# Cross-attention of a perceiver block: Newton steps on VectorE for the inverse roots, earlier loads of the second group's x, and a first group in two halves

## The chip, the cores and the metric

The kernel runs on one core of one Trainium2 chip. The metric is device time in microseconds (us) of one execution; the number compared is the median over several executions. The engines are named as the profile names them: PE (TensorE matmuls), PEld (TensorE weight loads), DVE (VectorE), ACT (ScalarE), POOL (GpSimd), SP (the queue that issues most DMAs).

## The reference

The block computes three residual steps on `x` of 128 batches x 32 rows x 512 columns, float32. The change lies in the first one alone: a layer norm of `x`, then cross-attention of each batch's 32 rows over 257 rows of context plus the 32 rows themselves.

```python
def _layernorm(x, axis=-1, eps=1e-05):
    m = jnp.mean(x, axis=axis, keepdims=True)
    v = jnp.var(x, axis=axis, keepdims=True)
    return (x - m) / jnp.sqrt(v + eps)

def _L0_xattn_ref(x, mask, k_cache, v_cache, wq, wk, wv, wo):
    q = jnp.einsum('bsd,ed->bse', x, wq)
    k_new = jnp.einsum('bsd,ed->bse', x, wk)
    v_new = jnp.einsum('bsd,ed->bse', x, wv)
    k = jnp.concatenate([k_cache, k_new], axis=1)
    v = jnp.concatenate([v_cache, v_new], axis=1)
    scale = 1.0 / math.sqrt(q.shape[-1])
    scores = jnp.einsum('bqd,bkd->bqk', q, k) * scale
    attn = jax.nn.softmax(scores, axis=-1)
    out = jnp.einsum('bqk,bkd->bqd', attn, v)
    return jnp.einsum('bqd,ed->bqe', out, wo)

x = x + _L0_xattn_ref(_layernorm(x), mask, ctx_2048, ctx_2048, wq, wk, wv, wo)
x = x + _L0_attn_ref(_layernorm(x), ...)   # delta-rule attention and an MLP
x = x + _L0_ffn_ref(_layernorm(x), ...)    # Hadamard FFN with quantised weights
```

## The kernel before

`perceiver_block` runs four stages one after the other: `cross_attention`, `delta_products`, `delta_out_mlp` and the Hadamard FFN. Only `cross_attention` is touched. It takes about the first 665 us of the span.

**Tiles and groups.** The 4096 rows of `x` are cut into 32 tiles of 128 rows (4 batches each), and the tiles into 8 groups of 4 (`SG = 512` rows). A tile's load is `load_x` (line 244, 256 KB). For each group `s` the normed rows are turned into `hT` (columns on partitions, 512 rows along the free axis), and `hT` is multiplied by `wq` and `wk` in 512-wide matmuls (line 437) into `qT` and `kT`. These are four output chunks `ec` of four partial products `dc` for each weight; every float32 matmul shows as two MATMUL records.

**One tile of attention.** For tile `n` the loop issues, in program order: `new_rows` (the tile's own values, L314, and the DMAs that put them beside the last context row in `vx`), `turned` (transposes of the softmax weights of tile `n-1`, L358), `project` of tile `n-2` (L395), `values` of tile `n-1` (L371 and L378, then the scaling `ao`, L383), `weights` of tile `n` (scores L336, maximum `nms` L341 and L342, exponential L346), and `flipped` (transposes of `ao`, L97). Context comes in two transfers of 2 MB a tile, `kall` for the keys (`load_keys`, L290) and `cx` for the values (`load_values`, L296), in two buffers each. A tile's `kall` is requested two tiles ahead, and a tile's `cx` one tile ahead, each as soon as the older buffer has been read.

**The norm of the next group.** `prepared(s + 1, ...)` is a generator that is advanced twice in each tile. Its steps for group `s+1` are: load of x tiles 0 to 2; an empty step; load of x tile 3 and mean and variance (L81, L82) of tiles 0 to 2; mean and variance of tile 3 and the inverse roots; the normed rows `xn` (L250) of the four tiles and their transposes (`across`: L97 on PE, then a copy into `hT` on ACT, L254). The inverse root is `deviation` (L258: a Sqrt activation on ACT over four columns) and a `reciprocal` on DVE (L276).

**The first group** has nothing to hide behind. It runs tile by tile, with the order on DVE written out by hand through `InOrder` (each instruction gets an edge to the one before it): statistics of tile `i`, Sqrt on ACT, then reciprocal, `xn` and transposes of tile `i-1`. Only then do the first matmuls with `wq` start.

**Order of the rest.** Outside `InOrder` the framework's scheduler sets each engine's order when the program is built: among the instructions that its own timing calls ready, the one that comes first in the program goes first. Beside the attention, `quantised_weights` reads the FFN's weights (`raw`, L192, 256 KB each), takes their absolute sums (L197) and rounds them (L212 to L214) on DVE; it is advanced four times a tile. DMAs of SP start in the order of its queue.

**The order of the initial loads** on SP is: x tiles of group 0, `wq`, `wk`, `wv`, `kall` and `cx` of tile 0, `wo`, `kall` and `cx` of tile 1.

Of the kernel before, what the change touches and what calls it, by code (L numbers as in the profile page):

```python
# [9 lines left out]

FP = mybir.dt.float32
BF = mybir.dt.bfloat16
AF = mybir.ActivationFunctionType
ALU = mybir.AluOpType
# [4 lines left out]
P = 128  # L19
D = 512  # L20
DC = D // P
NB = 128
T = 32
NT = NB * T
# [5 lines left out]
SG = 512  # L30
# [5 lines left out]
LN_EPS = 1e-5  # L36
RMS_EPS = 1e-6
Q_EPS = 1e-5
MAGIC = 12582912.0


def bc(ap, n):
# [15 lines left out]
class Ctx:  # L58


    def __init__(self, ctx, tc):
        self.tc, self.nc = tc, tc.nc
        nc = self.nc
        const = ctx.enter_context(tc.tile_pool(name="const", bufs=1))
        self.ident = const.tile([P, P], FP, name="ident")
        make_identity(nc, self.ident)
        self.identb = const.tile([P, P], BF, name="identb")
        nc.vector.tensor_copy(self.identb, self.ident)
        self.ones = const.tile([P, P], FP, name="ones")
        nc.vector.memset(self.ones, 1.0)  # L70
        self.ln_eps = const.tile([P, 1], FP, name="ln_eps")
        nc.vector.memset(self.ln_eps, LN_EPS)
        self.rms_eps = const.tile([P, 1], FP, name="rms_eps")
        nc.vector.memset(self.rms_eps, RMS_EPS)
        self.eps2 = const.tile([P, 1], FP, name="eps2")
        nc.vector.memset(self.eps2, LN_EPS * RMS_EPS)

    def mean_var(self, dve, pool, x, mv):

        st = pool.tile([P, 6], FP, name="bn_st")  # L80
        dve.bn_stats(st, x)  # L81
# [99 lines left out]
def quantised_weights(g: Ctx, pool, st, ps, out, weights):  # L181
# [3 lines left out]
    for (src, dst), sc in zip(weights, out):  # L185
# [23 lines left out]
        for i, piece in enumerate(pieces):  # L209
            t = load(piece)  # L210
            q = pool.tile([P, D], BF, name="qw")
            nc.vector.tensor_scalar(t, t, inv, 1.0, ALU.mult, ALU.min)  # L212
            nc.vector.tensor_scalar(t, t, -1.0, MAGIC, ALU.max, ALU.add)
            nc.vector.tensor_scalar(q, t, MAGIC, None, ALU.subtract)  # L214
            nc.gpsimd.dma_start(dst[:, i * D : (i + 1) * D], q)
# [3 lines left out]
def cross_attention(g: Ctx, x, ctx_kv, ctxT, wqT, wkT, wvT, woT, x1, stats, scales, ffn_weights):  # L219
# [5 lines left out]
    tc, nc = g.tc, g.nc  # L225
# [5 lines left out]
    with stack:  # L231
# [9 lines left out]
        def load_x(s, i):  # L241
            t = xp.tile([P, D], FP, name="xt")
            r = s * SG + i * P
            nc.sync.dma_start(t, x[r : r + P, :])
            return t

        def normed(dve, xt, mv, rstd):

            xn = wk.tile([P, D], FP, name="xn")
            dve.tensor_scalar(xn, xt, mv, rstd, ALU.subtract, ALU.mult)  # L250
            return xn

        def across(hT, i, xn):
            nc.scalar.copy(hT[:, :, i * P : (i + 1) * P], g.transposed(ps, xn, g.ident))  # L254

        def deviation(mv, n):
            rstd = st.tile([P, n], FP, name="rstd")
            nc.scalar.activation(rstd, mv[:, :, 1], AF.Sqrt, bias=g.ln_eps)  # L258
            return rstd

        def prepared(s, xt, hT):

            n = SG // P
            xt.extend(load_x(s, i) for i in range(n - 1))
            yield
            mv = st.tile([P, n, 2], FP, name="mv")
            yield
            xt.append(load_x(s, n - 1))  # L270
            for i in range(n - 1):
                g.mean_var(nc.vector, st, xt[i], mv[:, i, :])
            yield
            g.mean_var(nc.vector, st, xt[n - 1], mv[:, n - 1, :])
            rstd = deviation(mv, n)
            nc.vector.reciprocal(rstd, rstd)  # L276
            yield
            xn = []
            for i in range(n + 2):
                if 2 <= i:  # L280
                    across(hT, i - 2, xn[i - 2])
                if i < n:
                    xn.append(normed(nc.vector, xt[i], mv[:, i, 0:1], rstd[:, i : i + 1]))
                if i % 2:
                    yield

        def load_keys(gi):

            kall = cp.tile([P, DC, 4, NK], FP, name="kall")
            nc.sync.dma_start(kall[:, :, :, 0:LC], ctxT[gi])  # L290
            return kall

        def load_values(gi):
            b0 = gi * 4
            cx = cp.tile([P, 4, 2, D], FP, name="cx")
            nc.sync.dma_start(  # L296
                cx.rearrange("p b r d -> p b (r d)"),
                ctx_kv[b0 : b0 + 4, 0 : LC - 1, :].rearrange("b (p r) d -> p b (r d)", r=2),
            )
            return cx  # L300
# [102 lines left out]
        xt = [load_x(0, i) for i in range(SG // P)]  # L403
        kalls, cxs, quantised = {}, {}, None
        soft, out = None, None
        w = {}
        for n, src, wp in (("q", wqT, wp1), ("k", wkT, wp1), ("v", wvT, wp2), ("o", woT, wp3)):
            w[n] = wp.tile([P, DC, D], FP, name=f"w{n}")
            load_rows(nc, w[n], src)
            if n == "v":  # L410
                kalls[0] = load_keys(0)
                cxs[0] = load_values(0)
        kalls[1] = load_keys(1)
        cxs[1] = load_values(1)

        hT = sp.tile([P, DC, SG], FP, name="hT")
        dve = InOrder(tc, nc.vector)
        got = []
        for i in range(SG // P + 1):
            if i < SG // P:  # L420
                mv = st.tile([P, 1, 2], FP, name="mv0")
                g.mean_var(dve, st, xt[i], mv[:, 0, :])
                got.append((mv[:, 0, 0:1], deviation(mv, 1)))
            if i:
                mv, rstd = got[i - 1]
                dve.reciprocal(rstd, rstd)
                across(hT, i - 1, normed(dve, xt[i - 1], mv, rstd))
        for s in range(NT // SG):
            if s == NT // SG - 1:
                g.factors(*(t[:, 0:EARLY] for t in stats))  # L430
            qT = sp.tile([P, DC, SG], FP, name="qT", bufs=1)
            kT = sp.tile([P, DC, SG], FP, name="kT", bufs=1)
            for wn, dst in ((w["q"], qT), (w["k"], kT)):
                for ec in range(DC):
                    pp = ps.tile([P, SG], FP, name="ps")
                    for dc in range(DC):
                        nc.tensor.matmul(
                            pp, wn[:, dc, ec * P : (ec + 1) * P], hT[:, dc, :],
                            start=dc == 0, stop=dc == DC - 1,
                        )  # L440
                    (nc.vector.tensor_copy if ec % 2 else nc.scalar.copy)(dst[:, ec, :], pp)

            if quantised is None:
                quantised = quantised_weights(g, qp, st, ps, scales, ffn_weights)
            xt_next, hT_next, ahead = [], None, iter(())
            if s + 1 < NT // SG:
                hT_next = sp.tile([P, DC, SG], FP, name="hT")
                ahead = prepared(s + 1, xt_next, hT_next)
            for i in range(SG // P):
                n = s * (SG // P) + i  # L450
                kall = kalls.pop(n)
                vx = new_rows(n, kall, hT, kT, i)
                if soft is not None:
                    m, xm, vm, pr, rs = soft
                    prT = turned(pr)
                if out is not None:
                    project(*out)
                    out = None
                if soft is not None:
                    ao = values(cxs.pop(m), vm, prT, rs)  # L460
                    if n + 1 < NT // P:
                        cxs[n + 1] = load_values(n + 1)
                for _ in range(2):
                    next(quantised, None)
                next(ahead, None)
                got = weights(kall, qT, i)
                if n + 2 < NT // P:
                    kalls[n + 2] = load_keys(n + 2)
                if soft is not None:
                    out = m, xm, flipped(ao)  # L470
                for _ in range(2):
                    next(quantised, None)
                soft = n, xt[i], vx, *got
                next(ahead, None)
            xt, hT = xt_next, hT_next
# [2 lines left out]
        project(m, xm, flipped(values(cxs.pop(m), vm, turned(pr), rs)))  # L478


NG = NT // SG
GT = SG // P
GB = SG // T
H4 = 4
NC8 = H // H4
# [717 lines left out]
class HadamardFfn:  # L1203
# [5 lines left out]
    NG = IF // D  # L1209
# [66 lines left out]
    def open(self, ctx):  # L1276
# [22 lines left out]
    def first(self, ps):  # L1299
# [3 lines left out]
        for i in range(2):  # L1303
# [15 lines left out]
    def run(self):  # L1319
# [330 lines left out]
```

## Time and profile before

| what | us |
|---|---|
| three timed executions | 2870.92, 2873.64, 2877.52 |
| median | 2873.64 |
| the profiled execution, first to last instruction (its span) | 2872.8 |
| PE busy in the span | 2793.6 (97%) |
| DVE, ACT, POOL busy | 2016.4, 1037.3, 728.4 |
| mean granted TensorE clock | 0.992 of full speed |

The page gives no time for the profiled execution beside its span. The span lies 0.8 us under the median and inside the range of the three timed executions. "Granted clock" is the share of TensorE's full clock that the throttle let through. A row of a timeline has a start, a duration, the engine, the line in the kernel, the operation, output and inputs, a count, and in brackets the idle time of that engine before it with what ended the idle time.

### The profile page before, as it was taken

To read this page: it belongs to the slowest core of one execution; us is meant where nothing else is said; L and a number is where in the kernel's file an instruction comes from. 1 tells how busy PE (TensorE), PEld (TensorE's weight loads), DVE (VectorE), ACT (ScalarE), POOL (GpSimd) and SP (SyncE) were. 2 spreads that over 40 slices of the span, in tenths; PEclk is the share of its full clock that TensorE was granted. 3 is DMA by queue.
4 is the path that set the end of the run, shared out by engine and by line. 5 is a ranking of instruction groups with operands and counts; after the bars stand their busy time and mean duration, and the time that the engine had idled before them with its cause. 6 is when DMAs were issued, how large, how long until landed. Compare 5 with 4: busy or idle time off the path is not lost.

```text
span 2872.8 us, 45044 instructions
## 1 busy us (share of the span) xinstructions
PE 2793.6 (97%) x16863; PEld 1675.9 (58%) x16926; DVE 2016.4 (70%) x3371; ACT 1037.3 (36%) x1791; POOL 728.4 (25%) x1098
## 2 busy tenths in 40 slices
PE   8999999999999999899999999999999989999998
PEld 4444444444444444667676767677777656666665
DVE  2453544426599999778787777878622289999998
ACT  1111111215666666312222221111211146667665
POOL 2232323322687786221211121101100000000000
PEclk9999999999999999999999999999999999999999
DMA  9798998874555666641424231322221124443443
GB/s 325 260 328 303 347 334 287 298 250 120 160 145 143 185 181 186 188 130 58 133 62 129 67 124 54 120 85 65 95 88 34 35 76 88 88 87 83 85 82 76
DMA packets 347178, 429.80 MB, mean 150 GB/s; under 512 B 151888, under 2 KB 252624, under 8 KB 344528
## 3 DMA queue, kind: packets, MB, share of 16 engines
q1 hardware_dynamic: 305952, 324.36, 37.1%
q0 software_dynamic: 41008, 102.55, 11.7%
q8 instruction: 135, 2.21, 0.3%
q14 instruction: 83, 0.68, 0.1%
HBM read 288.88 MB, written 94.37 MB: 133 GB/s over the span
## 4 chain that ended last, share of the span: by engine, by line
PE 59%; DVE 13%; issue 2%; DMA 1%; SPq 0%; ACT 0%; POOL 0%; DVEq 0%; POOLq 0%; ACTq 0%
PE ps L151 19%; PE pm L1083 10%; PE pm L1086 9%; PE pm L1094 9%; PE pp L151 5%; PE ps L1057 4%; DVE acc L151 3%; PE ps L1026 2%; DVE W L151 2%; DVE pr L535 1%; DVE W L541 1%; DVE pr L151 1%; PE pg L151 1%; DMA xs<-x 1%; DVE m L151 1%
## 5 line engine op out<-in xcount | busy, mean ns | idle before, releaser
L1083 PE MATMUL pm<-hT,wg 128*128 128x256 f32 x1408 | 342.5, 385 | 0.2 <-ACT hT L1072 0.2
L1086 PE MATMUL pm<-hT,wu 128*128 128x256 f32 x1408 | 336.3, 382 | 1.3 <-DVE wu L1144 1.3
L1094 PE MATMUL pm<-wd,mT 128*128 128x512 f32 x704 | 307.4, 592 | 0.0
L1086 PEld LDWEIGHTS pm<-hT,wu 128*128 128x128 f32 x1408 | 269.3, 191 | 39.1 <-DVE wu L1144 1.6
L1083 PEld LDWEIGHTS pm<-hT,wg 128*128 128x128 f32 x1408 | 262.5, 191 | 50.3 <-issue 10.0
L535 DVE TENSOR_TENSOR pr<-L,W 128x960 f32<-128x960 f32 (+30 forms) x201 | 238.4, 1186 | 7.6 <-DMA L<-ld 3.8
L541 DVE TENSOR_TENSOR W<-W,pr 128x1024 f32<-128x1024 f32 (+30 forms) x202 | 241.3, 1195 | 2.3
L1094 PEld LDWEIGHTS pm<-wd,mT 128*128 128x128 f32 x704 | 132.4, 190 | 160.2 <-issue 160.0
L151 PE MATMUL ps<-wq,qT 128*128 128x512 bf16 x930 | 217.2, 381 | 4.6 <-ACT t L151 3.0
L1088 ACT ACTIVATE sg<-pm 128x256 f32<-128x256 f32 x176 | 67.3, 383 | 336.9 <-PE pm L1083 327.0
L1089 DVE TENSOR_TENSOR mT<-pm,sg 128x256 f32<-128x256 f32 x176 | 74.0, 421 | 143.0 <-PE pm L1086 141.2
L1420 POOL DMA_DIRECT2D xo<-x x31 | 26.3, 849 | 525.2 <-ACT xo L151 490.8
L323 POOL DMA_DIRECT2D vx<-vn x256 | 126.3, 500 | 118.7 <-DVE vn L319 92.5
L151 PEld LDWEIGHTS <-qT 128*128 128x128 bf16 x960 | 94.4, 98 | 105.0 <-issue 6.1
L151 DVE TENSOR_TENSOR mb<-m 128x1024 f32<-128x1024 f32 x128 | 153.3, 1219 | 0.1
L151 DVE TENSOR_TENSOR m<-mb 128x1024 f32<-128x1024 f32 x128 | 150.8, 1220 | 1.2
L151 ACT ACTIVATE t<-ps,magic,qs 128x512 f32<-128x512 f32 x158 | 115.6, 780 | 42.7 <-DVE qs L151 38.9
L151 PEld LDWEIGHTS ps<-hd,mT 128*128 128x128 f32 x1024 | 120.8, 194 | 6.9 <-ACT mT L151 2.8
L151 PE MATMUL ps<-hd,mT 128*128 128x128 f32 x1024 | 121.3, 277 | 2.3 <-ACT mT L151 2.3
L151 PE MATMUL pp<-hT,wv 128*128 128x512 f32 x256 | 120.3, 614 | 0.0
L579 POOL TENSOR_TENSOR kk<-kk,cm 128x256 f32<-128x256 f32 x128 | 118.4, 925 | 2.7
L151 PE MATMUL pp<-hT,wk 128*128 128x512 f32 x256 | 116.2, 596 | 1.9 <-ACT hT L151 1.9
(236 smaller groups left out, 4877.8 us busy)
## 6 DMA issues: line engine op xcount, KB each, us to landing
kall<-in_ctxT_dram SPq DMA_DIRECT2D x32, 2056.0 KB
cx<-in_ctx_dram SPq DMA_DIRECT2D x32, 2048.0 KB
x<-xo POOLq DMA_DIRECT2D x64, 256.0 KB, 3.6
ld<-kk POOLq DMA_DIRECT2D x128, 128.0 KB, 2.9
pd<-kk POOLq DMA_DIRECT2D x128, 128.0 KB, 2.7
L<-ld SPq DMA_DIRECT2D x32, 512.0 KB
pe<-pd SPq DMA_DIRECT2D x256, 64.0 KB
kqm<-kq SPq DMA_DIRECT2D x448, 32.0 KB
```

The lines of the kernel that those rows point to most:

```text
L151: got = method(*args, **kw)
L323: nc.gpsimd.dma_start(vx[r : r + T, j, :], vn[j * T : (j + 1) * T, halves[h]])
L535: self.dve.tensor_mul(pr[:, 0:n], bc(L[:, s, :, s + 1 : T].rearrange("p h t -> p t h"), HD), w[:, s].unsqueeze(1).to_broadcast([P, n, H4, ...
L541: self.dve.tensor_sub(w[:, s + 1 :], w[:, s + 1 :], pr[:, 0:n])
L579: nc.gpsimd.tensor_mul(q, q, cm.unsqueeze(1).to_broadcast([P, 2 * H4, T]))
L1026: last["pe"] = nc.tensor.matmul(po[a * 32 : (a + 1) * 32, c, :].rearrange("p (j t) -> p j t", t=T), m[:, 4 * c + a, e, :], q[:, :, 2 * a + ...
L1057: nc.tensor.matmul(pw, oT[:, i, dc, :], wo[:, dc, :], start=dc == 0, stop=dc == DC - 1)
L1083: nc.tensor.matmul(pg, wg[:, dc, fs], hT[:, dc, :], start=dc == 0, stop=dc == DC - 1)
L1086: nc.tensor.matmul(pu, wu[:, dc, fs], hT[:, dc, :], start=dc == 0, stop=dc == DC - 1)
L1088: nc.scalar.activation(sg, pg, AF.Silu)
L1089: mark[:] = [nc.vector.tensor_mul(mT[:, fc, :], pu, sg).ins]
L1094: nc.tensor.matmul(pd, mT[:, fc, i * P : (i + 1) * P], wd[:, fc, :], start=fc == 0, stop=fc == FC - 1,)
```

## The change

Three things change in `cross_attention`.

1. `deviation` and the reciprocal after it are replaced, for groups 1 to 7, by `inverse_root`: a seed from integer arithmetic on the bits of variance plus epsilon, and three Newton steps, all on DVE (13 instructions on 128x4). Group 0 keeps Sqrt and reciprocal.
2. The four x tiles of group 1 are loaded at the start, between `wo` and the `kall` and `cx` of tile 1. `prepared` loads only what is not there yet; for groups 2 to 7 it loads as before.
3. Group 0 is worked in two halves of two tiles: statistics, roots, normed rows and transposes of tiles 0 and 1, then their part of `qT` in matmuls of 256 columns, then the same for tiles 2 and 3. The order on PE, ACT and DVE is now written out through `InOrder` (the copies of `qT` out of PSUM are not part of it). `kT` of group 0, and both of the later groups, stay 512 wide.

```diff
-        def across(hT, i, xn):
-            nc.scalar.copy(hT[:, :, i * P : (i + 1) * P], g.transposed(ps, xn, g.ident))
-
-        def deviation(mv, n):
-            rstd = st.tile([P, n], FP, name="rstd")
-            nc.scalar.activation(rstd, mv[:, :, 1], AF.Sqrt, bias=g.ln_eps)
-            return rstd
+        def across(hT, i, xn, pe=None, act=nc.scalar):
+            act.copy(hT[:, :, i * P : (i + 1) * P], g.transposed(ps, xn, g.ident, pe=pe))
+
+        def projected(pe, dst, wn, hT, ts):
+            for ec in range(DC):
+                pp = ps.tile([P, ts.stop - ts.start], FP, name="ps")
+                for dc in range(DC):
+                    pe.matmul(
+                        pp, wn[:, dc, ec * P : (ec + 1) * P], hT[:, dc, ts],
+                        start=dc == 0, stop=dc == DC - 1,
+                    )
+                (nc.vector.tensor_copy if ec % 2 else nc.scalar.copy)(dst[:, ec, ts], pp)
+
+        def inverse_root(mv, n):
+            h = st.tile([P, n], FP, name="h")
+            y, t = (st.tile([P, n], FP, name=k) for k in ("rstd", "rt"))
+            nc.vector.tensor_scalar(h, mv[:, :, 1], LN_EPS, None, ALU.add)
+            nc.vector.tensor_single_scalar(t.bitcast(INT), h.bitcast(INT), 1, ALU.logical_shift_right)
+            nc.vector.tensor_scalar(y.bitcast(INT), t.bitcast(INT), -1, SEED, ALU.mult, ALU.add)
+            nc.vector.tensor_scalar(h, h, -0.5, None, ALU.mult)
+            for _ in range(3):
+                nc.vector.tensor_mul(t, y, h)
+                nc.vector.tensor_mul(t, t, y)
+                nc.vector.scalar_tensor_tensor(y, t, 1.5, y, ALU.add, ALU.mult)
+            return y

         def prepared(s, xt, hT):
             n = SG // P
-            xt.extend(load_x(s, i) for i in range(n - 1))
+            xt.extend(load_x(s, i) for i in range(len(xt), n - 1))
             yield
             mv = st.tile([P, n, 2], FP, name="mv")
             yield
-            xt.append(load_x(s, n - 1))
+            xt.extend(load_x(s, i) for i in range(len(xt), n))
...
             g.mean_var(nc.vector, st, xt[n - 1], mv[:, n - 1, :])
-            rstd = deviation(mv, n)
-            nc.vector.reciprocal(rstd, rstd)
+            rstd = inverse_root(mv, n)
...
                 cxs[0] = load_values(0)
+        second = [load_x(1, i) for i in range(SG // P)]
         kalls[1] = load_keys(1)
         cxs[1] = load_values(1)
...
-        dve = InOrder(tc, nc.vector)
-        got = []
-        for i in range(SG // P + 1):
-            if i < SG // P:
-                mv = st.tile([P, 1, 2], FP, name="mv0")
-                g.mean_var(dve, st, xt[i], mv[:, 0, :])
-                got.append((mv[:, 0, 0:1], deviation(mv, 1)))
-            if i:
-                mv, rstd = got[i - 1]
-                dve.reciprocal(rstd, rstd)
-                across(hT, i - 1, normed(dve, xt[i - 1], mv, rstd))
+        pe, act, dve = (InOrder(tc, e) for e in (nc.tensor, nc.scalar, nc.vector))
+        qT = sp.tile([P, DC, SG], FP, name="qT", bufs=1)
+        for half in range(2):
+            tiles = range(half * GT // 2, (half + 1) * GT // 2)
+            mvs = [st.tile([P, 2], FP, name="mv0") for _ in tiles]
+            roots = [st.tile([P, 1], FP, name="root") for _ in tiles]
+            for i, mv, root in zip(tiles, mvs, roots):
+                g.mean_var(dve, st, xt[i], mv)
+                act.activation(root, mv[:, 1:2], AF.Sqrt, bias=g.ln_eps)
+            for i, mv, root in zip(tiles, mvs, roots):
+                dve.reciprocal(root, root)
+                across(hT, i, normed(dve, xt[i], mv[:, 0:1], root), pe, act)
+            projected(pe, qT, w["q"], hT, slice(half * SG // 2, (half + 1) * SG // 2))
...
             kT = sp.tile([P, DC, SG], FP, name="kT", bufs=1)
+            if s:
+                qT = sp.tile([P, DC, SG], FP, name="qT", bufs=1)
+                projected(nc.tensor, qT, w["q"], hT, slice(0, SG))
+            projected(nc.tensor, kT, w["k"], hT, slice(0, SG))
...
-            xt_next, hT_next, ahead = [], None, iter(())
+            xt_next, hT_next, ahead = [] if s else second, None, iter(())
```

More of the change, by code (lines that the diff above doesn't have):

```diff
@@ L11 @@
 FP = mybir.dt.float32
+INT = mybir.dt.int32
 BF = mybir.dt.bfloat16
@@ L39 @@
 MAGIC = 12582912.0
+SEED = 0x5F3759DF
+NG = NT // SG
+GT = SG // P
 def bc(ap, n):
@@ L430, in cross_attention @@
                 g.factors(*(t[:, 0:EARLY] for t in stats))
-            qT = sp.tile([P, DC, SG], FP, name="qT", bufs=1)
             kT = sp.tile([P, DC, SG], FP, name="kT", bufs=1)
[L433 to L441, printed above, removed]
+            if s:
+                qT = sp.tile([P, DC, SG], FP, name="qT", bufs=1)
+                projected(nc.tensor, qT, w["q"], hT, slice(0, SG))
+            projected(nc.tensor, kT, w["k"], hT, slice(0, SG))
             if quantised is None:
                 quantised = quantised_weights(g, qp, st, ps, scales, ffn_weights)
-            xt_next, hT_next, ahead = [], None, iter(())
+            xt_next, hT_next, ahead = [] if s else second, None, iter(())
             if s + 1 < NT // SG:
@@ L478, in cross_attention @@
         project(m, xm, flipped(values(cxs.pop(m), vm, turned(pr), rs)))
-NG = NT // SG
-GT = SG // P
 GB = SG // T
```

## The prediction

> **What bounds the kernel now.** I read the page's busy table first, then the windows of 20 us over the first 760 us, then PE's own waits in the cross-attention, and last the timeline around the longest of them.
>
> The windows show who sets the pace of this stage. Columns: length, busy us and count of PE, PEld, DVE, ACT, POOL, then granted clock, DMA share, GB/s.
>
> ```profile
> 0.00:20.00 20.00, 12.66 (x31) 6.74 (x32) 5.90 (x23) 5.18 (x10) 0.70 (x6) 1.00 0.93 316
> ...
> 40.00:60.00 20.00, 19.54 (x144) 8.66 (x143) 8.77 (x22) 3.69 (x9) 10.48 (x20) 1.00 0.73 240
> 60.00:80.00 20.00, 15.65 (x112) 7.91 (x111) 9.73 (x22) 4.39 (x9) 4.49 (x9) 0.84 1.04 367
> ...
> 100.00:120.00 20.00, 20.00 (x47) 8.77 (x47) 4.58 (x8) 1.76 (x3) 0.00 (x0) 1.00 0.66 216
> ...
> 140.00:160.00 20.00, 17.35 (x177) 7.72 (x170) 13.34 (x37) 4.04 (x9) 11.35 (x22) 1.00 1.07 367
> ```
>
> PE is the bound: it is busy through whole windows, and ACT is nearly empty. DMA is full (share 1.04 to 1.07) while a group's tiles run, but has slack while `wq` and `wk` are applied (0.66). So time is won only where PE stands still or runs at a low clock, and lost where PE is made to wait. PE's own waits up to 680 us:
>
> ```profile
> PE ps L97 <- DVE xn L151: 6.7, 3, 6.0
> PE ps L97 <- DVE xn L250: 6.1, 4, 4.3
> PE ps L358 <- ACT pr L346: 3.8, 3, 1.6
> PE ps L97 <- DVE ao L383: 2.8, 4, 0.8
> ```
>
> The first is the start. The second is the normed rows of a next group: four times, 4.3 us once and 0.6 us in three others (groups 2, 4 and 6). The change can shorten these two rows, and lengthen the second and fourth. The long one, in the timeline:
>
> ```profile
> 71.42 0.67 DVE L197 TENSOR_REDUCE sums<-raw 128x1 f32<-128x512 f32 x1
> 72.00 0.68 DVE L81 BATCH_NORM_STATS2 bn_st<-xt 128x6 f32<-128x512 f32 x1
> ...
> 73.39 0.30 ACT L258 ACTIVATE rstd<-mv,ln_eps 128x4 f32<-128x4 f32 x1 [0.61 <-DVE mv L82]
> 73.73 0.18 DVE L276 RECIPROCAL rstd<-rstd 128x4 f32<-128x4 f32 x1 [0.23 <-ACT rstd L258]
> 73.94 1.00 DVE L250 TENSOR_SCALAR xn<-xt,mv,rstd 128x512 f32<-128x512 f32 x2
> 74.54 1.97 PE L97 MATMUL ps<-ident,xn 128*128 128x128 f32 x8 [4.35 <-DVE xn L250]
> ```
>
> And a window of 4 us right after it:
>
> ```profile
> 76.00:80.00 4.00, 4.00 (x8) 1.93 (x7) 1.97 (x4) 0.86 (x2) 0.00 (x0) 0.50 1.02 413
> ```
>
> The statistics of x tile 3 stand in DVE's order behind the softmax and the reductions of tile 2, because that tile was requested only at 60.17. Five steps in a row follow, and PE has nothing else in its order. The window shows the second price: after the stall PE runs at half clock. The windows of one us put the low clock from 73.5 to 80.4.
>
> **Early x (part 2).** The chain for group 1 no longer waits for a load late in tile 1: statistics, root and `xn` take 3.7 us (0.68 + 0.17 + a root of 2.3, below, + 0.55), and x has landed long before 46 us, where tile 1 begins. So the 4.35 us go, and so does the low clock: PE works from 74.54 to 80.37 at 0.50, 5.8 us that hold 2.9 us of full-speed work. Gain: 4.35 + 2.9 = 7.3 us. By the Trainium skill (TensorE: Matmul & The Clock Gate, Part 1) activity is judged in free-running windows of 3.41 us. The 6.8 us at 0.50 here are two such windows, and a shorter stall could by that rule cost none.
>
> What is late next? The four loads are 1.05 MB, at 385 GB/s 2.7 us, put ahead of `kall` and `cx` of tile 1. By their packets these end at 34.4 and 40.1 now, so at 37.1 and 42.8; they are read at 55.1 (L336) and 65.0 (L371). `vx` of tile 0 moves from about 41 to 44 and is read at 53.0. All covered by 9 us or more. `kall` of tile 3 ends at 73.8 and is read at 89.1, then at 81.8: still covered. On SP the x issues leave 31.43 (3.77 us) and 60.17 (1.38 us), so that the transfers behind them start no later.
>
> **Group 0 in halves (part 3).** The first `wq` matmul starts at 11.51, released by the last copy of `hT`. Tiles 0 and 1 alone are transposed by 8.5 and copied by about 8.9. But the completion events of the `wq` load in the trace end at 9.86, so the start moves to 9.9: gain 1.6 us. Against it: the eight transposes of tiles 2 and 3 now stand between the halves (0.66 us for four at full clock in `flipped`, so 1.3), and before the second half PE again waits for the last `hT` copy, as it does now (0.68 <- ACT hT L254): 0.7. Narrow matmuls are nearly free: start to start the trace has 0.216 us for 256 columns (L1083) and 0.429 for 512 (L437), so 64 x 0.216 = 13.8 against 32 x 0.429 = 13.7. And the clock: the first nine MATMULs run at half speed (0.855 us instead of 0.429) and full speed comes at 15.5, four us after the dense work starts. If it comes at the same moment, 1.6 us more work is done at half speed: 0.8 us lost. Sum -1.6 + 1.3 + 0.7 + 0.1 + 0.8 = +1.3; if the clock rises 3.4 us earlier (the trace's low-clock records last 3.4 or 6.8 us), +1.3 - 1.7 = -0.4. I take +0.5.
>
> **Newton on DVE (part 1).** ACT loses seven Sqrt (0.30 us each) and 14 table loads: L258 has eight now and L346 nine; one and two remain. 14 x 1.283 = 18.0 us of an engine that is busy 36%. The load that looks closest to the path, 159.86 to 161.14 ahead of the exponential, ends 3 us before PE needs the result (L358 at 164.14, behind 3.6 us of L314). Worth 0 on the path; if that cover went, at most 1.3 us a group. The Trainium skill (ScalarE: Activation LUTs, What ACT_TABLE_LOAD costs) prices a switch at 2.66 us with a drain of 1.38; here the exponential starts 0.01 us after the load ends. By the page 37 us of ACT would go, and the sum would be the same by either, as all of it lies beside the path.
>
> DVE gains 13 instructions and loses one. No row has this chain; the nearest are TENSOR_SCALAR on 128x1 (0.152, in another line 0.214), TENSOR_TENSOR on 128x1 (0.140) and a gap of 0.03 between dependent ones (L341 to L342). 13 x 0.18 = 2.3 us, ends 13 x 0.14 = 1.8 and 13 x 0.21 = 2.8. The path it replaces, from the end of the aggregate to `xn`, is 0.5 us. So roots of groups 2 to 7 come 1.8 us later. Queued behind it on DVE are the two `ao` scalings, `nms` and `xn`; PE waits for `ao` and `xn`. The scores have cover: the exponential's chain has 2.2 us to spare ahead of L358, and 1.3 more without the load.
>
> What that costs hangs on PE's order. PE has 3.6 us of work that needs neither, the eight L314 of the next tile. Where the scheduler sees the root late it puts these first; then not only is nothing lost, the present waits of groups 2, 4 and 6 (0.48 + 0.60, 0.77 + 0.59, 0.78 + 0.59, together 3.8 us) can vanish. Where it keeps the order, 1.8 us are lost on the even groups and 1.2 on the odd ones (PE arrives 0.6 us after `xn` there): 9.0 us. Ends: -3.8 and +9.0. I take half of the gain, -1.9, because the chain is long enough to be seen, while 1.8 us less than 3.6 of free work covers it.
>
> **Sum:** -7.3 + 0.5 - 1.9 = -8.7 us. From the profiled execution, 2872.8 - 8.7 = 2864.1; from the median, 0.8 above it, 2864.9: I say 2865. After 665 us nothing is touched, so the rest only moves earlier.
>
> **Rivals.** (a) *The stall goes and Newton gives most of it back*: PE keeps its order; -7.3 + 0.5 + 9.0 = +2.2, so 2876; with half of the 9.0, 2871. For it: the 0.6 us waits show that the order is set by a timing that differs from the chip's. Against: 2 us is more than such a slip. (b) *Slower*: the 13 instructions come earlier in the program than `ao` and run as one block ahead of it, so PE stands at the end of L336 for 2.3 us, six times 2.3 = 13.8: -7.3 + 0.5 + 13.8 = +7.0, 2880.6. It decides from (5.7 + 6.8) / 6 = 2.1 us a group. A stall that also halves the clock, as the 4.35 us one did, adds 2.9 each. Against it: `ao` already had DVE work ahead of it (0.48 us waits), and PE's L314 can go first. (c) *The stall stays*: the scheduler still puts group 1's statistics behind tile 2's softmax although x is there, or the wait moves on; then 0 + 0.5 and at best -1.9: about 2873. Against: statistics of tiles 0 to 2, whose x was there, ran at 50 to 53 us, in tile 1.
>
> **How the numbers follow.** Forecast 0.53, its own range 2862 (all of the 3.8 us and the early clock) to 2870 (none of them, +1.3 at the start); (a) 0.20; (b) 0.17; (c) 0.10. No change is what lies within 0.2%, 5.7 us, about what a measurement of this kernel can tell: 2867.9 to 2879.4. Of the forecast 0.44 lies below that and 0.09 inside; (a) gives 0.17 inside and 0.03 above, (b) 0.02 above for its milder half beside 0.15 of its own, and (c) 0.08 inside and 0.02 above: 0.44, 0.34, 0.22. The range 2857 to 2883 leaves out the stalls with a low clock above and, below, a group's other waits (L358, 3.8 us) going too.
>
> **What would show it.** Right: in the changed profile no PE wait over 1 us for `xn` L250, no clock under 0.9 between 60 and 85 us, tile 3's first L314 at about 70 instead of 76.3; L258 with no table load beyond the first group's; first `wq` matmul at 9.9 and first `wk` matmul at 27 to 28.7 instead of 27.32. Wrong: PE waits on `ao` or `xn` of 1 to 2.5 us at groups 2 to 7, or L314 of tile 3 not ahead; a root chain on DVE outside 1.8 to 2.8 us; PE waiting at L336 or L371 for a DMA.

## The result, and the profile after

The changed kernel takes 2890.68 us (median; 2887.56 to 2894.00), the kernel before beside it 2874.9: a ratio of 1.0056, 95% interval [1.0042, 1.0069]. The forecast was 2865 us, and the range ended at 2883. The profiled execution has a span of 2888.6 us, 15.8 us more than before, and nearly all of it lies in the cross-attention: the first matmul of the next stage starts 13.6 us later.

The busy table of the changed kernel, its first line (busy us, share of the span, number of instructions):

```profile
PE 2798.9 (97%) x16958; PEld 1682.3 (58%) x16958; DVE 2027.5 (70%) x3457; ACT 1016.7 (35%) x1772; POOL 730.5 (25%) x1098
```

ACT lost 20.6 us of work, and no time was won by it. The windows of the changed kernel, with the columns used before:

```profile
0.00:20.00 20.00, 11.09 (x37) 9.20 (x38) 6.44 (x24) 4.16 (x9) 0.70 (x6) 1.00 0.93 315
60.00:80.00 20.00, 20.00 (x130) 9.50 (x128) 9.21 (x21) 4.23 (x12) 7.01 (x15) 1.00 1.03 358
140.00:160.00 20.00, 14.32 (x106) 6.33 (x103) 9.82 (x32) 2.06 (x6) 7.10 (x14) 0.91 1.04 363
160.00:167.00 7.00, 4.76 (x12) 3.12 (x13) 5.56 (x19) 2.11 (x6) 0.33 (x1) 0.51 0.91 333
```

From 60 to 80 us the aim is reached: PE is full, and the clock is 1.00 where it was 0.84. The price stands at 140 to 167 us, one group later: PE idle for 5.7 us of the first 20 (2.65 before), and then the clock at 0.51. PE's own waits up to 680 us name who holds it (engine, tile, line, waited for: total us, times, longest):

```profile
PE ps L101 <- DVE xn L254: 9.3, 6, 2.7
PE ps L380 <- ACT pr L368: 8.9, 4, 3.5
PE ps L155 <- DVE root L155: 5.9, 1, 5.9
PE ps L101 <- DVE ao L405: 3.4, 4, 1.8
PE ps L155 <- DMA wq<-in_x_wqT_dram: 3.0, 1, 3.0
```

Before, the normed rows cost 6.1 us, nearly all in one stall, and the exponential 3.8. That stall is gone, yet both totals are larger: `xn` now has three waits of 2.5 to 2.7 us, at groups 2, 4 and 6, and the exponential waits of up to 3.5. The timeline of group 2's root:

```profile
158.55 0.22 DVE L274 TENSOR_SCALAR h<-mv 128x4 f32<-128x4 f32 x1
158.61 0.48 DVE L405 TENSOR_SCALAR ao<-ps,rs 128x256 f32<-128x256 f32 x1
...
159.14 0.44 PE L101 MATMUL ps<-ident,ao 128*128 128x128 f32 x2 [1.78 <-DVE ao L405]
...
159.77 0.16 DVE L279 TENSOR_TENSOR rt<-rstd,h 128x4 f32<-128x4 f32 x1
159.97 0.16 DVE L280 TENSOR_TENSOR rt<-rt,rstd 128x4 f32<-128x4 f32 x1
160.15 0.51 ACT L368 ACTIVATE pr<-ps,nms 128x289 f32<-128x289 f32 x1
160.16 0.16 DVE L281 SCALAR_TENSOR_TENSOR rstd<-rt,rstd 128x4 f32<-128x4 f32 x1
...
161.44 0.16 DVE L281 SCALAR_TENSOR_TENSOR rstd<-rt,rstd 128x4 f32<-128x4 f32 x1
161.63 1.00 DVE L254 TENSOR_SCALAR xn<-xt,mv,rstd 128x512 f32<-128x512 f32 x2
...
162.24 1.97 PE L101 MATMUL ps<-ident,xn 128*128 128x128 f32 x8 [2.66 <-DVE xn L254]
...
164.00 2.77 PE L336 MATMUL ps<-wv,hT 128*128 128x512 f32 x3
```

Instructions that depend on each other start 0.20 us apart, each 0.16 long. With the scalings and the maximum between them the 13 last from 158.55 to 161.60, 3.05 us. PE has `new_rows` (L336) to do and could do it at once, but does it after the transposes of `xn`: its order is not the one that the forecast hoped for.

### The profile page after: what moved, and what is told of

It reads as the page before. It is cut to its first block, busy times and chain, and to the rows that moved or that the text cites. A ratio compares the mean times of both kernels' runs of the same rounds, so it can differ in the third digit from the quotient of the medians.

```text
span 2888.6 us, 45237 instructions
## 1 busy us (share of the span) xinstructions
PE 2798.9 (97%) x16958; PEld 1682.3 (58%) x16958; DVE 2027.5 (70%) x3457; ACT 1016.7 (35%) x1772; POOL 730.5 (25%) x1098
## 3 DMA queue, kind: packets, MB, share of 16 engines
q0 software_dynamic: 41008, 102.55, 11.4%
## 4 chain that ended last, share of the span: by engine, by line
PE 78%; DVE 12%; DMA 5%; issue 3%; SPq 1%; ACT 1%; POOL 0%; DVEq 0%; ACTq 0%; POOLq 0%
PE ps L155 19%; PE pm L1100 10%; PE pm L1103 9%; PE pm L1111 9%; PE ps L264 7%; PE pp L155 5%; PE ps L1074 4%; PE ps L417 3%; PE ps L336 3%; DVE acc L155 3%; PE ps L1043 2%; DVE W L155 1%; PE ps L358 1%; PE ps L101 1%; PE ps L393 1%
## 5 line engine op out<-in xcount | busy, mean ns | idle before, releaser
L417 PE MATMUL ps<-wo,aoT 128*128 128x512 f32 x256 | 118.1, 605 | 1.5 <-ACT aoT L410 1.5
```

The costliest lines, as they stand in the source:

```text
L417: nc.tensor.matmul(po, aoT[:, dc, :], w["o"][:, dc, :], start=dc == 0, stop=dc == DC - 1)
```

## The experiments

Each kernel is compared with the kernel before, run beside it on the same chip. "Lead" below is how far PE is ahead (minus) or behind at one instruction, against the profile of before. Two things were disputed: why the root costs so much, and where the 7.3 us of early x went.

### The parts alone

**e1**: the kernel before with the Newton root (part 1 of the change) alone. **e2**: early x (part 2) alone. **e3**: the halves (part 3) alone. **e4**: the changed kernel with Sqrt and reciprocal put back:

```diff
-            rstd = inverse_root(mv, n)
+            nc.scalar.activation(rstd, mv[:, :, 1], AF.Sqrt, bias=g.ln_eps)
+            nc.vector.reciprocal(rstd, rstd)
```

> The kernel before with the Newton root alone (x of group 1 late, group 0 whole). PE's order is the one of before; on DVE the 13 instructions stand between the statistics and the normed rows. Theory N (the root's chain is the loss): the wait of PE for xn grows by about 2 us at each of groups 1 to 7, by 1.9 where PE already waited and by 0.5 to 0.7 where it did not, and a longer wait halves the clock at least once more (1.7 to 3.4 us each): +10 to +16 us. Theory R (the loss is DVE standing on raw transfers once x is early): +2 to +5 us, raw waits of PE at L358 as before (1.1 to 1.6 us).

> The kernel before with the early x alone. Theory N: the stall at 70 to 74 us and the half clock after it go, -7.3 us less what the later groups shift, so -8 to -5 us. Theory R: PE, now 7 us ahead, meets late raw transfers in group 1 (PE waits of 2 to 3.5 us at the transposes of the softmax weights, with low clock), which give back 3 to 8 us: -4 to +1 us.

> The kernel before with group 0 in halves alone. Both theories: the start alone moves, first wk matmul at 28.5 to 29.6 us instead of 27.3, nothing after it changes: +1 to +2.5 us.

> The changed kernel with Sqrt and reciprocal in place of the Newton root. Theory N: nearly all of the loss goes, the rest is -7.3 +2.2 and a reorder of 1 us: -6 to -3 us against before. Theory R: the raw waits and low clocks at about 147 and 224 us stay, 0 to +5 us.

Measured: e1 1.0074 [1.0057, 1.0092], some 21 us slower; e2 1.0003 [0.9993, 1.0014]; e3 1.0000 [0.9988, 1.0013]; e4 1.0017 [1.0007, 1.0028]. e1 lies above both of its ranges; e2 and e4 lie in those of theory R; e3 shows nothing of its +1 to +2.5 us, which its interval does not exclude. So the root costs 21 us alone and 11 on top of the other two (1.0056 against 1.0017), and early x brings nothing although its stall is gone. PE's waits of e1 between 85 and 640 us:

```profile
PE ps L101 <- DVE xn L254: 9.2, 6, 2.5
PE ps L380 <- ACT pr L368: 7.8, 4, 2.6
```

The kernel before has 1.8 and 3.8 in these rows. That is 11.4 us more, 7.4 for `xn` and 4.0 for the exponential, and the wait for `xn` at group 1, ahead of this window, is 6.26 us instead of 4.35. With it goes the clock: low-clock records in the stage add up to 27.3 us at 0.50, against 6.8, which is another 10 us. Together this is some 23 of the 27.1 us by which PE is behind at the end of the stage in this profile. (The whole profiled execution is only 16.6 us longer than the one of before: behind the stage it has 16.8 us of low-clock records, the other 39.8.) Compared instruction by instruction, PE's order in e1 is the one of before: transposes of `xn`, then `new_rows`.

### The root and PE's order

**f1** is the kernel before with the transposes of `xn` 0 and 1 put behind `new_rows` of tile 3. **f2** is the same with the Newton root, and **g3** is the changed kernel with it:

```diff
                 vx = new_rows(n, kall, hT, kT, i)
+                if i == SG // P - 1:
+                    next(ahead, None)
...
                 soft = n, xt[i], vx, *got
-                next(ahead, None)
+                if i != SG // P - 2:
+                    next(ahead, None)
```

> The kernel before (Sqrt and reciprocal, x of group 1 late, group 0 whole); the one edit: the transposes of xn 0 and 1 of the next group are issued behind new_rows of tile 3, no longer at the end of tile 2, so that PE has the eight L314 matmuls (3.6 us) ahead of them. Theory P (PE's order is fixed by the program, and PE stands at the transposes of xn until the root chain ends): the 4.35 us stall of group 1 shrinks to below 1 us and loses its low clock, the three waits of 0.6 us go; -5 to -10 us against before. Theory D (what counts is the time that DVE itself spends, or a later resource gives everything back): the wait moves to another line, and the time stays within 3 us of before.

> The kernel before with the Newton root, and with the same late transposes of xn 0 and 1. Newton alone cost about 21 us. Theory P: the eight L314 matmuls cover the 2.6 us of the 13 instructions; no PE wait of 2.46 us for xn is left, and the time is 0 to 6 us above f1, so at or below before. Theory D: the added DVE time costs the same wherever PE's transposes stand: 12 to 21 us above f1, with waits of 1 to 3 us on ao, on the maximum's exponential (L346) or on the scores' inputs in place of those for xn.

> The changed kernel with one edit: the transposes of xn 0 and 1 of the next group are issued behind new_rows of tile 3. Newton on top of early x and halves cost about 10 us in the runs before this one. Theory P (PE's order makes the Newton chain cost): the four waits of 2.46 us for xn and their low clocks go, and the time falls from 0.56% above before to 0 to 0.2% above it, where early x with halves and Sqrt stood. If instead the Newton chain costs by DVE time once x is early: it stays 0.4% or more above.

Measured: f1 0.9993 [0.9980, 1.0005], f2 0.9990 [0.9978, 1.0001], g3 1.0005 [0.9993, 1.0017]. With PE's work in this order the Newton root costs nothing that stands out of the noise: f2 is not above f1, and the changed kernel gets back nearly all it lost. Theory P, that PE's fixed order made the root costly, holds; theory D, that DVE's own time did, falls. The timeline of f2 at the same root:

```profile
158.11 0.22 DVE L274 TENSOR_SCALAR h<-mv 128x4 f32<-128x4 f32 x1
...
160.05 2.74 PE L336 MATMUL ps<-wv,hT 128*128 128x512 f32 x6
...
161.16 0.16 DVE L281 SCALAR_TENSOR_TENSOR rstd<-rt,rstd 128x4 f32<-128x4 f32 x1
161.36 1.00 DVE L254 TENSOR_SCALAR xn<-xt,mv,rstd 128x512 f32<-128x512 f32 x2
...
162.63 1.04 PE L101 MATMUL ps<-ident,xn 128*128 128x128 f32 x8
```

The chain is as long as before (3.2 us), and the row of the transposes has no wait: PE worked on L336 meanwhile. Not every wait for `xn` is gone. At group 1 of f2, where x still comes late, PE waits 3.63 us (6.26 in e1), and at group 2 of g3 1.87 us. f1 missed on its own gain: 8.4 us ahead at tile 3, it fell back to 1.9 behind by the end of the stage. Between 85 and 640 us it has no wait for `xn`, but 6.8 us of waits for `ao` and 5.6 us for the exponential; where such waits come from is taken up next.

### Where the gain of early x goes

In e2 PE is 7.5 us ahead at 82 us and level at 240 us. Some 1.3 us go at once and without a wait: from 74.31 to 85.01 PE takes 10.70 us for the 101 matmuls that took 9.42 before, and scores and products with `vx` now alternate there. PE's first wait stands at the maximum of group 1's last tile. The timeline of e2 there:

```profile
136.59 0.39 SPq L310 DMA_DIRECT2D cx<-in_ctx_dram  x1
137.09 0.60 SPq L196 DMA_DIRECT2D raw<-in_f_w_gateT_dram  x1
137.58 0.46 DVE L355 TENSOR_REDUCE nms<-ps 128x1 f32<-128x289 f32 x1 [0.31 <-PE ps L350]
142.34 0.49 DVE L216 TENSOR_SCALAR raw<-raw,inv 128x512 f32<-128x512 f32 x1 [4.31 <-DMA raw<-in_f_w_gateT_dram]
142.75 0.15 DVE L356 TENSOR_SCALAR nms<-nms 128x1 f32<-128x1 f32 x1
142.99 0.50 ACT L360 ACTIVATE pr<-ps,nms 128x289 f32<-128x289 f32 x1 [4.21 <-DVE nms L356]
143.64 0.55 PE L372 MATMUL ps<-ident,pr 128*128 128x128 f32 x3 [2.10 <-ACT pr L360]
```

Between the two instructions of the maximum stands a rounding step of the FFN's weights, and it waits 4.31 us for its `raw`; the last one ahead of it went out at 137.09, right behind 2 MB of `cx`. The exponential and then PE wait with it. The row was there before (2.72 us on DVE, 1.55 on PE): a PE that comes earlier finds `raw` still on its way and waits longer. Here that is little, and at 152 us PE is 6.2 us ahead. Two waits take the rest. One is of the same kind, at 217.61: 2.23 us on PE, behind 4.18 us in which DVE stood for `raw`; before, there was none. The other is for `xn` of group 2, 3.24 us where it was 0.60, with a low clock of 3.41 us:

```profile
150.32 0.88 DVE L397 TENSOR_SCALAR ao<-ps,rs 128x256 f32<-128x256 f32 x2 [1.98 <-PE ps L392]
151.11 0.48 DVE L216 TENSOR_SCALAR raw<-raw,inv 128x512 f32<-128x512 f32 x1
...
153.03 0.69 DVE L85 BATCH_NORM_STATS2 bn_st<-xt 128x6 f32<-128x512 f32 x1
...
155.38 1.01 DVE L254 TENSOR_SCALAR xn<-xt,mv,rstd 128x512 f32<-128x512 f32 x2
...
155.99 1.97 PE L101 MATMUL ps<-ident,xn 128*128 128x128 f32 x8 [3.24 <-DVE xn L254]
```

In this one DVE stands for no DMA. It works without a pause from 150.32 on, and most of two rounding steps (from 151.11) comes ahead of the statistics that `xn` needs. Before, these steps stood ahead of `ao`, from 154.16 on. So part of the loss is the place of the steps in DVE's order, and not a wait. The runs that follow move, thin out, take away or unbind these steps.

**f3**: early x, and the four steps of a tile behind its maximum. **f4**: f3 with the late transposes.

```diff
-            nc.vector.tensor_scalar_mul(nms, nms, scale)
+            mark[0] = nc.vector.tensor_scalar_mul(nms, nms, scale).ins
...
-                for _ in range(2):
-                    next(quantised, None)
+                for _ in range(4):
+                    with tc.issue_after(mark[0]):
+                        next(quantised, None)
```

> The kernel before with x of group 1 loaded early, and with the four steps of the FFN's weights of each tile put behind the tile's maximum (L342) on DVE. Early x alone took the stall away (about 7.5 us by 80 us of the span) and gave it back by 220 us, in PE waits of 2.1 to 3.2 us at which DVE stood on the sums or the rounding of raw. Theory Q (the order on DVE gives it back): those waits go, and the time is 4 to 8 us below before. Theory M (the DMA engines are full there, so the same time is lost at the next transfer): PE waits for kall, cx or x instead, and the time is within 2 us of before.

> Early x, late transposes of xn 0 and 1, and the FFN's weights behind the tile's maximum, with Sqrt and reciprocal. Theories P and Q together: no PE wait over 1 us for xn or for the exponential in groups 1 to 7, few low-clock records in the stage; 8 to 14 us below before. Theories D or M: within 3 us of before.

Measured: f3 1.0067 [1.0049, 1.0085], f4 1.0099 [1.0084, 1.0115]. Both expectations fell, the rivals' too: DVE stood for `raw` and `qw` 136 us between 85 and 640 us in f3 (42 in e2, 40 before), 61 of them for the write-out of `qw`. Four steps in one go use up the three buffers of `raw` and the two of `qw`. Whether the steps matter at all, or the DMA engines are full anyway, was told apart by **g1**, early x with all 96 steps behind the last tile:

```diff
-                for _ in range(2):
-                    next(quantised, None)
...
         project(m, xm, flipped(values(cxs.pop(m), vm, turned(pr), rs)))
+        for _ in quantised:
+            pass
```

> Early x with Sqrt, and none of the FFN weights' 96 steps inside the tiles: they are issued behind the last tile, so the whole takes longer; what is read is when the cross-attention's PE work ends in the span (before: 665 us). Theory W (raw and what stands behind it on SP and DVE takes the gain of early x back): without raw in the tiles no PE wait over 1 us is left behind group 1 and the offset of -7.5 us against before at 80 us of the span is kept or grows; the last new_rows L314 comes 7 to 20 us earlier than before. Theory M (context, x and the rest fill the DMA engines by themselves): the offset goes back to within 3 us of zero by 250 us all the same.

The whole takes 3008.26 us (one execution), since the steps now come last. In the stage the lead is 8.9 us at 240 us and grows to 17.2 by 484, and it stays there to 640. PE's longest waits up to 700 us in g1 (the first line is the start):

```profile
PE ps L101 <- DVE xn L155: 7.2, 3, 6.2
PE ps L101 <- DVE ao L397: 2.3, 2, 1.5
PE ps L409 <- ACT aoT L402: 1.5, 2, 0.7
PE ps L385 <- ACT prT L374: 0.9, 2, 0.5
```

No wait for `xn` of a later group and none for the exponential. The DMA engines are as full as ever in the tiles (share 1.05 from 125 to 165 us and 1.06 from 205 to 245), but PE waits for none of these transfers: theory M falls, and the weights' steps take the gain back. The next runs looked for a better place for them. **g2**: early x, two steps a tile and six behind each projection. **g4**: the same with Newton and late transposes. **h2**: three steps a tile.

```diff
+            for _ in range(6 if s else 0):
+                next(quantised, None)
             xt_next, hT_next, ahead = [] if s else second, None, iter(())
...
-                for _ in range(2):
-                    next(quantised, None)
+                next(quantised, None)
```

> Early x with Sqrt; the FFN weights' steps are two a tile instead of four, and six more behind the wq and wk projections of groups 1 to 7, where the DMA share is 0.66 and DVE is a quarter busy. Theory W: the waits on raw go out of the tiles, and the gain of early x stays: 5 to 12 us below before. Theory M: within 2 us of before. If the raw loads delay the x loads behind them on SP, waits for xn or statistics of 1 us and more come instead and it is 0 to 5 us above before.

> Newton root, early x, late transposes of xn 0 and 1, and the FFN weights' steps spread as in the run before (two a tile, six behind each projection); group 0 whole. Theories P and W together: no PE wait over 1 us for xn or for the exponential in groups 1 to 7; 6 to 14 us below before. Theory M: within 3 us of before.

> Early x with Sqrt; three steps of the FFN's weights a tile instead of four (96 steps over all 32 tiles, the last group included, instead of 24 tiles). Theory W2: a quarter less in each tile takes about a quarter to a half of the loss, and the last group gets what it did not have: 2 to 6 us below before. Theory W1: the landing of raw sets it, so nearly as much: 2 to 5 us below before. If only where in a tile the steps stand decides: within 2 us of before.

Measured: g2 1.0012 [0.9999, 1.0025], g4 1.0018 [1.0003, 1.0032], h2 1.0024 [1.0013, 1.0036]. All three missed (g2's 3.4 us lie in the range of its last case, but the waits are for `ao`, not for `xn`). In g2 and g4 PE is 5.7 and 7.4 us ahead at 149 us and loses 7 to 8 us in the two tiles behind the projections of groups 2, 4 and 6, where the last steps of the six still stand ahead of `ao` (PE waited 17.1 us for it in g2). DVE's waits for `raw` and `qw` are longer than in e2: 60, 59 and 55 us.

So these places are no better. The next runs are aimed at the waiting itself. **h1**: early x and six buffers of `raw`. **h3**: all of Newton, early x, late transposes, three steps a tile, six buffers.

```diff
-            t = pool.tile([P, D], FP, name="raw", bufs=3)
+            t = pool.tile([P, D], FP, name="raw", bufs=6)
```

> Early x with Sqrt; raw has six buffers instead of three, so that its loads are issued and land further ahead of the steps on DVE that read them; the steps stay where they are. Theory W1 (DVE stands for raw's landing, since its load goes out only when a buffer is free): the waits for the exponential at 143 and 217 us shrink below 1 us, the offset of -7.5 us at 80 us is kept past 250 us, and the time is 4 to 10 us below before. Theory W2 (it is raw's transfer itself, on engines that context and x fill in the tiles, or the DVE time of the steps, whenever they are issued): within 3 us of before.

> Newton root, early x, late transposes of xn 0 and 1, three steps of the FFN's weights a tile, six buffers of raw; group 0 whole. Theories P with W1: 8 to 15 us below before, no PE wait over 1 us in groups 1 to 7. P with W2: 2 to 6 us below before, with waits of 1 to 3 us left for the exponential or ao in some groups.

Measured: h1 1.0016 [1.0002, 1.0030], h3 1.0047 [1.0030, 1.0063]. Still slower, and outside every range given, but h1 shows why. The wait for the exponential fell from 7.9 to 0.2 us, as expected of more buffers, and waits for `ao` of up to 5.9 us took its place. DVE's row for the write-out of `qw` grew to 17.9 us in h1 and 36.2 in h3, from 11.0 in e2. The timeline of h1 ahead of such a wait:

```profile
298.45 0.88 DVE L218 TENSOR_SCALAR qw<-raw 128x512 bf16<-128x512 f32 x2 [3.74 <-DMA fq<-qw]
299.18 1.07 POOL L219 DMA_DIRECT2D fq<-qw  x2 [5.85 <-DVE qw L218]
...
304.21 0.43 DVE L218 TENSOR_SCALAR qw<-raw 128x512 bf16<-128x512 f32 x1 [2.87 <-DMA fq<-qw]
304.79 0.43 DVE L218 TENSOR_SCALAR qw<-raw 128x512 bf16<-128x512 f32 x1 [0.15 <-DMA fq<-qw]
```

The last operation of a step writes `qw`, of which there are two; a third must wait until an older one has been written out, 5.0 us after its issue. The last runs give both plenty. **i1**: early x, seven buffers of each. **i2**: that with the steps behind the maximum (f3's order). **i3**: that with the late transposes (f4's).

```diff
-            t = pool.tile([P, D], FP, name="raw", bufs=3)
+            t = pool.tile([P, D], FP, name="raw", bufs=7)
...
-            q = pool.tile([P, D], BF, name="qw")
+            q = pool.tile([P, D], BF, name="qw", bufs=7)
```

> Early x with Sqrt; seven buffers of raw (three before) and seven of the rounded weights qw (two before). Theory W3 (DVE stands, in order, for two DMAs of each step: raw's landing and the write-out that frees qw; three and two buffers bring both onto it): with both in plenty the waits of DVE for raw and qw between 85 and 640 us, some 37 us with early x alone, fall below 12, and the time is 4 to 10 us below before. Theory W2 (the DMA engines' time or the steps' own DVE time): within 3 us of before.

> As the run before this, with the four steps of each tile behind the tile's maximum on DVE. With three and two buffers this order cost 21 us more than before, and DVE stood 136 us for raw and qw. Theory W3: it was those DMAs; with seven of each DVE's waits for raw and qw fall below 30 us and the time falls by 20 to 30 us, to 0 to 10 us below before. Theory W2 or an order that is bad in itself: it stays 10 us and more above before.

> As the run before this, with the late transposes of xn 0 and 1 as well (that order cost 28 us with three and two buffers). Theory W3: 3 to 14 us below before, with no PE wait for xn over 1 us in groups 1 to 7. Theory W2: 10 us and more above before.

Measured: i1 0.9977 [0.9964, 0.9990], i2 0.9965 [0.9953, 0.9976], i3 0.9964 [0.9952, 0.9975]: 2870.55, 2868.08 and 2867.32 us where the kernel before took 2877.89 beside them. The times are as theory W3 had them, and theory W2 falls: f3's kernel, 0.67% slower with few buffers, is 0.35% faster with many, and f4's goes from 0.99% slower to 0.36% faster, with the same DVE work and the same transfers. DVE's waits in e2 between 85 and 640 us:

```profile
DVE qw L218 <- DMA fq<-qw: 11.0, 3, 5.0
DVE raw L216 <- DMA raw<-in_f_w_gateT_dram: 7.6, 4, 4.3
DVE sums L201 <- DMA raw<-in_f_w_upT_dram: 7.0, 3, 4.2
```

and the same view of i2:

```profile
DVE raw L216 <- DMA raw<-in_f_w_upT_dram: 6.1, 3, 3.5
DVE raw L216 <- DMA raw<-in_f_w_downT_dram: 6.0, 2, 3.6
DVE sums L201 <- DMA raw<-in_f_w_downT_dram: 4.4, 2, 2.4
```

The row of `qw` is gone altogether in i1, i2 and i3. What remains, 21 to 32 us in all, is the landing of `raw`; the 12 us expected of i1 were missed. From h1 to i1, `qw` got five more buffers and `raw` one, and the time fell by some 11 us.

Two things are mixed in this. With more buffers the scheduler also sets another order on DVE: in the tile around 205 us e2 has four reductions of `raw` between `xo` and the maximum, the last of them 4.18 us late, and i1 has five, the last 1.24 us late. No run has the one without the other. And the wait for `xn` of group 2 is untouched by buffers: 3.24 us in e2 and h1, 3.28 in i1. It falls to 0.85 us where the steps stand behind the maximum (f3, i2), and to none with the late transposes as well (i3). So buffers and the place of the steps both count.

PE's lead in the profiles, minus for ahead: at `turned` of tile 2 (81.77 us before), at `new_rows` of tile 11 (239.38) and at the next stage's first matmul (675.13).

| kernel | ratio | tile 2 | tile 11 | end |
|---|---|---|---|---|
| changed | 1.0056 | -5.3 | +9.6 | +13.6 |
| e1 Newton alone | 1.0074 | +2.9 | +13.1 | +27.1 |
| e2 early x alone | 1.0003 | -7.5 | +0.4 | +4.2 |
| f2 Newton, late transposes | 0.9990 | -2.1 | -0.6 | -1.1 |
| f3 early x, steps behind maximum | 1.0067 | -7.2 | +9.2 | +25.4 |
| i3 f4 with seven buffers each | 0.9964 | -7.9 | -5.0 | -6.0 |

Every kernel with early x is 5 to 8 us ahead at tile 2; what differs is whether it keeps it. A single profile's end and the ratio need not agree to the microsecond, since the low clocks behind this stage differ from run to run (17 to 50 us of records).

Left open: no run has the kernel before with seven buffers and late x, so how the 0.35% divides between buffers and early x is not known; nor one of the Newton root with seven buffers.

## Why the prediction was wrong

Forecast -8.7 us, measured +16. By e4 and the changed kernel the gap of 24.8 us divides into 13.1 for the root (-1.9 forecast, +11.2 measured on top of the rest) and 11.7 for early x with the halves (-6.8 forecast, +4.9 measured).

- **PE's order: the step that failed.** "Where the scheduler sees the root late it puts these first", and then half of a gain. It did not: PE's order is the same with either root. The forecast had an end for that, +9.0 us, and took the other side. f2 and g3 show that this one order was the cost of the root, as far as the noise lets one see.
- **The price of a kept order** was too low as well, 9.0 against e1's 21. Not for the waits it counted: those for `xn` behind group 1 grew by 7.4 us in e1, to 2.46 us at each even group and 0.5 to 0.8 at the odd ones, although the chain took 3.05 us at group 2 of the changed kernel and not 2.3 (pitch 0.20, and other work between). The sum left out the clock: rival (b) had "2.9 each" for it, rival (a) and the end of +9.0 had none. e1 lost about 10 us that way, and 4.0 us more in waits for the exponential.
- **Early x: right for the stall itself, -7.3 forecast,** -7.5 at 82 us in e2 (-6.2 from 85 us on); no `xn` wait at group 1 and a clock of 1.00 there.
- **"What is late next?" was the second failed step.** It followed the landings of `kall`, `cx` and `vx`, found 9 us of cover, and put the sum at nothing. It did not ask what else stands in DVE's order: the weights' steps, which wait for their own DMAs with few buffers and, at group 2, stand ahead of the statistics. e2 ended level with before, and e4 4.9 us behind it. The prediction's own page shows the exponential's waits (3.8 us); they were not followed back to `raw`.
- **The start** was put at +0.5. In the changed profile the first `wk` matmul comes 2.2 us later (29.52), since `wq` was ready at 10.85 and not at 9.9, and the full clock came at 16.7 instead of 15.5; in e3 it was 0.5 later, and the median shows nothing. ("The first nine MATMULs" at half speed is a misreading: five start ahead of 15.5, 0.853 us apart. The sum does not use the count.)
- **ACT: right.** 20.6 us less work against 20.1 worked out, worth nothing on the path.
- **Rivals.** (a) had the mechanism of the root, but +2.2 us in all where +16 came. (b) had the sign but not the mechanism: DVE ran `ao` (158.61) right behind the first Newton instruction; the 1.78 us wait for it has rounding steps and statistics ahead of it. Of (c) the stall did not stay, but its other half, "or the wait moves on", is what e2 shows: nothing of the gain was left.

## What to carry to other kernels

A longer chain on an engine that is not the bound costs what the bound's engine has put behind it: read the order of that engine in the trace, and do not count on a scheduler to reorder it; if independent work is there, put it first by hand. Before counting a removed stall as won, follow the other engines' in-order queues to the next DMA wait: an instruction that waits for a buffer or a landing holds all behind it, and an engine that comes earlier only meets it earlier. Side work of that kind needs enough buffers at both of its ends, and its place in the order still has to be looked at where it stands ahead of what the bound's engine waits for.

## What the runs showed of the hardware

**Short stalls cost clock.** In the profiles of all these kernels, between 60 and 660 us, every PE wait of 2.6 us or more came with a low-clock record of 3.41 or 6.83 us: waits of 6.26 us (e1, group 1) and 4.35 us (the kernel before) with 6.83. Between 1.9 and 2.6 us it went either way. In e1 waits of 2.46 us at 167.97 and 505.77 came with 3.41 and one at 335.97 with 6.83, but the changed kernel's two of 2.46 us (332.54 and 496.48) with none; one of 2.01 us there (224.39) came with 3.41, one of 2.23 (e2, 217.61) with none. What decides is not shown. Where the record came, it cost 1.7 to 3.4 us more. The Trainium skill (TensorE: Matmul & The Clock Gate, HAM oscillation — how this bites in real kernels) gives as the abstract rule that PE should have no idle gap over some 3.4 us; here gaps of 1.9 to 2.6 us could be enough.

**Tiny dependent operations on DVE** of 128x4 take 0.16 us and start 0.20 us apart. The Trainium skill (VectorE: DVE Perf Modes, Rules for kernel authors) says of chained operations to keep their number small; the 13 here agree, at 2.4 us with nothing between them (e1, 75.05 to 77.44), where Sqrt and reciprocal took 0.5.

**A write-out under load**: 128 KB from POOL freed its buffer 5.0 us after its issue (h1, 299.18 to 304.21), while the DMA share was 1.08. By the fit in the Trainium skill (DMA: Bandwidth & Descriptors, Anatomy of one DMA — SWDGE (gpsimd) path) it would be an estimated 2.0 + 131072/436e3 = 2.3 us.
